# Another order of the first stages of a two-layer kernel of seven-product matrix multiplications

## The chip, the cores and the metric

The kernel runs on one core of a Trainium2 chip. The metric is the device time of one execution in microseconds (us); lower is better. One execution was also taken with the hardware profiler, and all durations below come from it. TensorE (PE) multiplies, VectorE (DVE) adds, ScalarE (ACT) scales and copies, GpSimd (POOL) and SyncE (SP) issue transfers.

## What is computed

Eight samples of 256 tokens with 1024 features go through two layers, each added to its input. Layer 0 multiplies by a matrix that depends on the sample: the common W plus the sample's mask turned into signs, times the sample's coefficient. Layer 1 picks one of eight matrices by an index.

```python
def reference(x, condB_coeff, itok_B_3_7, mask, L0_cond_W, L0_cond_b, L1_cond_weight):
    # layer 0; x is (8, 256, 1024), mask is (8, 1024, 1024) of 0 and 1
    sign = 2 * mask - 1
    y = x + einsum('bsi,oi->bso', x, L0_cond_W) + L0_cond_b \
          + einsum('bsi,bio->bso', x, sign) * condB_coeff[:, None, None]
    # layer 1
    w = L1_cond_weight[itok_B_3_7]              # (8, 1024, 1024)
    return y + einsum('bsi,boi->bso', y, w)
```

All of it is float32.

## The kernel before

**Stages.** One layer of one sample is a stage; there are 16. A 256 x 1024 by 1024 x 1024 multiplication is cut into 2 x 2 blocks on all sides and done with seven block products in place of eight (p1 to p7, in the way of Strassen and Winograd). For this, sums of blocks are formed first: s1 to s4 of the tokens (128 x 512 each, small) and t1 to t4 of the weights (a whole block each, 128 x 2048). A product is four steps of 128 in depth and fills one PSUM bank; in the profile every float32 matmul stands as two instructions. TensorE does the products of a stage in the order p1, p5, p6, p2, p7, p3, p4. Several products gather in the same bank ("u", "v", "w"); after p1 and after p6 ScalarE copies bank u out (`keep`), since later products go on adding to it, and VectorE adds banks and copies into R, the buffer of the result (`add`, L682 before).

**Layer 0** needs its matrix made: a mask block is loaded, ScalarE scales it (L525), VectorE adds the block of W (L539, "fold" in this text). R of the sample is loaded with x, and POOL adds the bias to it with an accumulating transfer (L428). When R holds y, VectorE transposes it in squares of 32 (L449) and ScalarE moves the squares to their places (L463, 16 instructions for each half), because y with features on partitions is the next stage's token operand. **Layer 1** needs no making: its four blocks are loaded as they are, by an index read on SP (L521).

**Stage 0** (layer 0 of sample 0) is done differently, without the seven products, while everything is loading: mask and W come in 11 pieces, are scaled (L308) and folded (L316), and 64 matmuls with the weights stationary give y with features on partitions (L323). ScalarE prepares x plus bias (`bias_first`, L341, eight instructions), and VectorE adds it to the four banks and so evicts them (`evict_first`, L350).

**Stage 1** was layer 1 of sample 0, the `flipped` stage: weights stationary, tokens moving in pieces of 128 columns, sixteen matmuls per product (L608). Its result comes out with features on partitions, like y, so y is added as it lies, and the sample is stored to its own output `out0`. Stages 2 and 3 are layer 0 of samples 1 and 2; from then on layer 1 of one sample and layer 0 of a later one take turns. All stages from 2 on have the tokens stationary (L618).

**What sets the order.** All work is described as tasks with a guessed length, and `plan` runs them once in a model: each engine takes, of the tasks that are ready, the one that is due first, where due times are counted back from the times at which TensorE's products should begin (HEAD = 34.5 us, then 3.435 us per product). The instructions are written out in the order of the model's starting times. On the chip each engine works its own queue strictly in that order; a wait holds up all that is behind it. Loads go through SP's queue, with eight in flight at most; weights have 11 buffers, R has 3.

Of the kernel before, what the change touches and what calls it, by code (L numbers as in the profile page):

```python
# [30 lines left out]
ORDER = ("p1", "p5", "p6", "p2", "p7", "p3")  # L31

# [16 lines left out]
LOAD, STORE, LATENCY, BEGIN = 2.50, 0.60, 2.2, 1.7  # L49
# [33 lines left out]
def plan(tasks, room, may_take):  # L83

    followers = {t: [] for t in tasks}
    for t in tasks:
        for u in t.after:
            followers[u].append(t)
    for t in reversed(tasks):
        due = [f.latest for f in followers[t]]  # L90
        own = t.latest + t.length if t.latest is not None else 1e9
        t.latest = min(due + [own]) - t.length - t.latency
    waiting = {t: len(t.after) for t in tasks}
    ready = {}
    for t in tasks:
        ready.setdefault(t.engine, [])
        if not waiting[t]:
            ready[t.engine].append(t)
    free_at = dict.fromkeys(ready, 0.0)
    free_at["DMA"] = BEGIN  # L100
    left = {}
    events, now, done = [(BEGIN, None)], 0.0, 0
    while done < len(tasks):
        for engine, queue in ready.items():
            if free_at[engine] > now + 1e-9:
                continue
            for t in sorted(queue, key=lambda t: t.latest):
                if t.earliest > now + 1e-9:
                    events.append((t.earliest, None))
                elif all(room[r.pool] > 0 for r in t.takes) and may_take(t):  # L110
                    queue.remove(t)
                    for r in t.takes:
                        room[r.pool] -= 1
                        left[r] = r.users
                    t.start, t.end = now, now + t.length + t.latency
                    free_at[engine] = now + t.length
                    if t.moves:
                        free_at["DMA"] = max(now, free_at["DMA"]) + t.moves
                        events.append((free_at["DMA"], None))
                    events += [(t.end, t), (free_at[engine], None)]  # L120
                    break
        assert events, "the plan is stuck"
        now = min(e[0] for e in events)
        for e in [e for e in events if e[0] <= now + 1e-9]:
            events.remove(e)
            t = e[1]
            if t is None:
                continue
            done += 1
            for r in t.uses:  # L130
                left[r] -= 1
                if not left[r]:
                    room[r.pool] += 1
            for f in followers[t]:
                waiting[f] -= 1
                if not waiting[f]:
                    ready[f.engine].append(f)
    order = {t: i for i, t in enumerate(tasks)}
    return sorted(tasks, key=lambda t: (round(t.start, 6), order[t]))
# [3 lines left out]
def kernel(  # L143
# [17 lines left out]
    out0: bass.AP,  # L161
# [72 lines left out]
    stages = [(0, 0), (1, 0), (0, 1)]  # L234
    for b in range(2, B):
        stages += [(0, b), (1, b - 1)]
    stages.append((1, B - 1))

    HEAD = 34.5
    owed = [0] + [3 if s == 1 else 2 for s in range(1, len(stages))]  # L240
    next_load = [0]
    loads: list[Task] = []

    def may_take(t) -> bool:
        s = getattr(t, "stage", None)
        if s is None:
            return True
        if t.engine == "DMA":
            if loads[next_load[0]] is not t:
                return False  # L250
            if room["w"] - 1 < sum(owed[: s + 1]):
                return False
            next_load[0] += 1
        else:
            owed[s] -= 1
        return True
# [132 lines left out]

    order = [(n, k, cols) for n, (k, cols) in enumerate(pieces[:-2])]  # L390
    order += [(len(pieces) - KC + k, k, ds(j * H, H)) for j in range(2) for k in (KC - 2, KC - 1)]
    last_mm = None
    mm_half = {}
    for i, (n, k, cols) in enumerate(order):
# [5 lines left out]
            takes=list(first.values()) if i == 0 else [],  # L400
            uses=([] if i == 0 else list(first.values())) + [m[k // 2], x0],
# [3 lines left out]
        mm_half[cols.start // H] = last_mm  # L405
# [33 lines left out]
    def turn(j: int, source, after, target: Buffer, opens: bool, view, moved: list):  # L439
# [25 lines left out]
        for n in range((P // Q) ** 2):  # L465
# [8 lines left out]
                    uses=[r] if takes else [r, target],  # L474
                )
# [3 lines left out]
    def stage(s: int):  # L479
        nonlocal last_mm  # L480
        layer, b = stages[s]
        final = s + 1 == len(stages)
        begin = HEAD + (s - 1) * 7 * PRODUCT
# [3 lines left out]
        if layer == 0:  # L487
            A = Buffer("a")
            got = [
                task(  # L490
                    "DMA",
                    LOAD,
                    lambda: nc.sync.dma_start(out=take(A)[:, 0:4], in_=xT[b - 1]),
                    takes=[A],
                    latency=LATENCY,
                    earliest=begin - 7 * PRODUCT,
                )
            ]
# [3 lines left out]
        flipped = s == 1  # L502
        apart = Buffer("turn")

        def part(name: str):
            if flipped and name == "s3":
                return (apart.tile if apart.tile is not None else take(apart))[:, 0].rearrange(
                    "p (k n) -> p k n", k=KH
                )
# [3 lines left out]
        def load(q: str):  # L513
            t = take(W[q])
            if layer == 0:
                nc.sync.dma_start(out=t.bitcast(I32), in_=mask[b - 1, block(q)])
# [3 lines left out]
            rows = w1_blocks[ds(rows0[b] + block(q), 1)]  # L520
            nc.sync.dma_start(out=t, in_=rows.rearrange("n p k o -> (n p) k o"))  # L521

        def scale(q: str):
            t = W[q].tile
# [4 lines left out]
        for q in BLOCKS:  # L529
            W[q] = Buffer("w")  # L530
            t = task("DMA", LOAD, lambda q=q: load(q), takes=[W[q]], latency=LATENCY)
            t.stage = s
            loads.append(t)
            if layer == 0:
                t = task("ACT", SCALE, lambda q=q: scale(q), after=[t], uses=[W[q]])
                t = task(
                    "DVE",
                    BLOCK,
                    lambda q=q: v.tensor_tensor(W[q].tile, W[q].tile, w0[q], ALU.add),  # L539
                    after=[t],  # L540
                    uses=[W[q]],
                )
            done[q] = t
        ready_r = load_r(b, begin) if layer == 0 else None

        def sum_of(what: str, after=()):
            left, op, right = SUMS[what]
            if what[0] == "s":
# [5 lines left out]
                    takes=[apart] if flipped and what == "s3" else [],  # L554
# [4 lines left out]
            fresh = what in ("t2", "t3") or (what == "t1" and s == 1)  # L559
# [26 lines left out]
        if s == 1:  # L586
            sum_of("t1")
            sum_of("t2", got)
            sum_of("t3", got)
# [11 lines left out]
        def product(name: str, a: str, w: str, bank: Buffer, opens: bool, cols=slice(0, H)):  # L601
            t = bank.tile if bank.tile is not None else take(bank)
            if flipped:
                for c in range(KH):
                    for k in range(KH):


                        nc.tensor.matmul(  # L608
                            out=t[:, ts(c, TH)],
                            lhsT=W[w].tile[:, k, ts(c, P)],  # L610
                            rhs=part(a)[:, k],
                            start=opens and c == 0 and k == 0,
                            stop=k == KH - 1,
                            skip_group_check=True,
                        )
                return
# [9 lines left out]

        def add_product(name: str, after=()):
            nonlocal last_mm
            a, w = PRODUCTS[name]
            bank = BANK[name]  # L630
# [5 lines left out]
            if flipped and a == "a11":  # L636
                needed = got[:2]
# [6 lines left out]
                uses=[A, W[w]] + ([] if opens else [r]) + ([apart] if flipped and a == "s3" else []),  # L644
# [19 lines left out]
        if flipped:  # L664
            state = {q: yT[b][1][-1] for q in BLOCKS}
# [3 lines left out]
        begun: list[str] = []  # L669

        def add(q: str, r: Buffer, op, after, get=lambda r: r.tile):
            t = R[b]
            opens = flipped and not begun
            from_y = flipped and q not in begun
            begun.append(q)

            def emit():
                to = (take(t) if opens else t.tile)[:, block(q)]
                left = to
                if from_y:  # L680
                    left = A.tile[:, block(q)].rearrange("p k n -> p (k n)")
                v.tensor_tensor(to, left, get(r), op)  # L682

# [3 lines left out]
                emit,  # L687
                after=[state[q], after, *gate, *([state[begun[0]]] if flipped and not opens else [])],
                takes=[t] if opens else [],
                uses=([] if opens else [t]) + [r] + ([A] if from_y else []),  # L690
                latest=begin + (len(mm) + 1.5) * PRODUCT,
# [10 lines left out]
        def store(q: str, cols, queue=None):  # L702
# [6 lines left out]
                    out=out0[:, block(q)] if flipped else out[b - 1, :, int(q[0]) - 1, lo:hi],  # L709
# [8 lines left out]
        copies: dict[str, tuple] = {}  # L718
# [172 lines left out]
```

## Time and profile before

| | before |
|---|---|
| time, median of 3 runs | 402.2 us (402.19 to 402.61) |
| profiled execution | 402.02 us, span 400.2 us |
| granted TensorE clock | 0.999 |
| TensorE busy | 394.2 us, 98% |
| VectorE busy | 330.6 us, 83% |
| ScalarE busy | 184.2 us, 46% |
| moved by DMA | 103.00 MB, mean 257 GB/s |

The span runs from the first to the last instruction. Busy time of TensorE includes time in which a matmul stands in the pipeline. "Start to start" is the distance of two instructions that follow each other without a gap; it is a little shorter than the duration of one. In a timeline the columns are start and length in us, engine and line, operation, operands, count, and in brackets the idle time of the engine before it with what ended it.

### The profile page before, as it was taken

The numbers are of one execution on the slowest core, as the hardware profiler recorded it, in microseconds if no ns is written. First come the engines' busy times: TensorE is split into PE (matmuls) and PEld (weight loads), VectorE is DVE, ScalarE is ACT, GpSimd is POOL, SyncE is SP. The second block draws the span as 40 slices with busy tenths as digits, with TensorE's granted clock in tenths as the row PEclk, the third lists the DMA queues.
The fourth block names the chain that finished last, engine by engine and source line by source line (L and its number), as shares of the span: only waits on it lengthen the run. The fifth ranks groups of instructions, "written<-read, shape, count | busy, mean of one in ns | idle before, by whom it ended". The sixth has DMA issues, their size and how long they took to land.

```text
span 400.2 us, 3444 instructions
## 1 busy us (share of the span) xinstructions
PE 394.2 (98%) x1155; PEld 200.0 (50%) x1155; DVE 330.6 (83%) x307; ACT 184.2 (46%) x305; POOL 27.2 (7%) x44
## 2 busy tenths in 40 slices
PE   7999999999999999999999999999999999999996
PEld 4889994444444444444444444444444444444443
DVE  2347999999999999799968998789977999668132
ACT  4552635205951496970079510993119920391000
POOL 0100011100101101010010100102001020001101
PEclk9999999999999999999999999999999999999999
DMA  8999999997873739958399573987659694601102
GB/s 256 404 414 422 418 347 388 379 338 311 189 335 111 309 113 378 318 172 317 119 397 286 209 316 125 374 236 290 235 211 345 183 376 146 273 41 53 54 0 106
DMA packets 19298, 103.00 MB, mean 257 GB/s; under 512 B 2320, under 2 KB 2832, under 8 KB 9808
## 3 DMA queue, kind: packets, MB, share of 16 engines
q1 hardware_dynamic: 14688, 87.24, 56.4%
q0 software_dynamic: 4448, 15.47, 14.6%
q8 instruction: 9, 0.15, 0.2%
q10 hardware_dynamic: 144, 0.07, 0.1%
q14 instruction: 9, 0.07, 0.1%
HBM read 94.38 MB, written 8.39 MB: 257 GB/s over the span
## 4 chain that ended last, share of the span: by engine, by line
PE 94%; DMA 4%; DVE 0%; SPq 0%; issue 0%; DVEq 0%
PE ps L618 84%; PE ps L608 6%; PE ps L323 4%; DMA w<-mask 2%; DMA w_sb<-w0T 2%; DVE w L316 0%; SPq L279 0%; SPq L286 0%; SPq L288 0%; DVE r L767 0%; DVEq L316 0%
## 5 line engine op out<-in xcount | busy, mean ns | idle before, releaser
L618 PE MATMUL ps<-w,a 128*128 128x512 f32 (+1 forms) x792 | 336.7, 588 | 0.0
L618 PEld LDWEIGHTS ps<-w,a 128*128 128x128 f32 x792 | 149.9, 190 | 186.7 <-issue 182.7
L569 DVE TENSOR_TENSOR w<-w,w 128x2048 f32<-128x2048 f32 (+1 forms) x61 | 136.8, 2252 | 3.4 <-PE ps L618 2.1
L463 ACT ACTIVATE a<-turn 32x256 f32<-32x256 f32 x224 | 92.7, 414 | 69.6 <-DVE turn L449 66.7
L539 DVE TENSOR_TENSOR w<-w,w_sb 128x2048 f32<-128x2048 f32 x28 | 64.0, 2288 | 6.1 <-ACT w L525 6.1
L682 DVE TENSOR_TENSOR r<-r,ps 128x512 f32<-128x512 f32 x73 | 49.1, 681 | 23.7 <-PE ps L618 23.5
L525 ACT ACTIVATE w<-w,cn_sb,c_sb 128x2048 f32<-128x2048 int32 x28 | 58.5, 2092 | 19.6 <-DMA w<-mask 18.8
L552 DVE TENSOR_TENSOR a<-a 128x512 f32<-128x512 f32 x59 | 39.4, 688 | 0.4
L654 ACT ACTIVATE s<-ps 128x512 f32<-128x512 f32 x15 | 8.8, 590 | 58.5 <-PE ps L618 51.2
L323 PE MATMUL ps<-a,w 128*128 128x256 f32 x128 | 29.1, 384 | 1.6 <-DMA a<-x0a 0.7
L708 POOL DMA_DIRECT2D out<-r x31 | 17.0, 549 | 199.6 <-DVE r L682 199.5
L323 PEld LDWEIGHTS ps<-a,w 128*128 128x128 f32 x128 | 23.8, 190 | 6.8 <-DVE w L316 3.1
L654 ACT ACTIVATE u<-ps 128x512 f32<-128x512 f32 x15 | 8.9, 594 | 36.7 <-PE ps L618 36.5
L316 DVE TENSOR_TENSOR w<-w,w_sb 128x512 f32<-128x512 f32 (+2 forms) x13 | 10.5, 815 | 15.6 <-DMA w_sb<-w0T 11.9
L608 PE MATMUL ps<-a,w 128*128 128x128 f32 x192 | 21.8, 275 | 0.0
L608 PEld LDWEIGHTS ps<-a,w 128*128 128x128 f32 x192 | 21.7, 192 | 0.1
L449 DVE STREAM_TRANSPOSE turn<-r 128x512 f32<-128x512 f32 x28 | 19.6, 707 | 0.6
L428 POOL DMA_DIRECT2D r<-bias x7 | 8.7, 1245 | 158.0 <-DMA r<-xR 158.0
L308 ACT ACTIVATE w<-w,cn_sb,c_sb 128x512 f32<-128x512 int32 (+2 forms) x13 | 11.6, 909 | 14.7 <-DMA w<-mask 14.7
L682 DVE TENSOR_TENSOR r<-r,s 128x512 f32<-128x512 f32 x14 | 9.6, 685 | 6.6 <-ACT s L654 6.6
L682 DVE TENSOR_TENSOR r<-r,u 128x512 f32<-128x512 f32 x14 | 9.6, 687 | 3.5 <-ACT u L654 3.4
L813 PE MATMUL idle<-zeros 128*128 128x512 bf16 (+1 forms) x11 | 3.6, 503 | 1.2 <-DVE warm L808 1.2
(24 smaller groups left out, 22.9 us busy)
## 6 DMA issues: line engine op xcount, KB each, us to landing
w<-w1T SPq DMA_DIRECT2D x32, 1024.0 KB, 9.2
w<-mask SPq DMA_DIRECT2D x28, 1024.0 KB, 10.1
out<-r POOLq DMA_DIRECT2D x31, 256.0 KB, 7.4
r<-xR SPq DMA_DIRECT2D x7, 1024.0 KB, 7.6
a<-xT SPq DMA_DIRECT2D x7, 1024.0 KB, 6.4
r<-bias POOLq DMA_DIRECT2D x7, 1024.0 KB, 15.6
w<-mask SPq DMA_DIRECT2D x5, 512.0 KB, 8.5
w_sb<-w0T SPq DMA_DIRECT2D x5, 512.0 KB, 9.0
```

The costliest lines, as they stand in the source:

```text
L323: nc.tensor.matmul(out=t.rearrange("p (c n) -> p c n", c=half)[:, c % half], lhsT=m_view(k)[:, ts(oc, P)], rhs=x0_view()[:, k], start=k == ...
L449: lambda t=t, opens=not turned: v.transpose(out=(take(r) if opens else r.tile)[:, t], in_=view(source.tile)[:, 2 * t + j]),
L463: nc.scalar.activation(to[:, :, :, f], src[:, :, :, g], AF.Copy)
L525: nc.scalar.activation(t, t.bitcast(I32), AF.Identity, bias=cn_sb[:, b : b + 1], scale=c2_sb[:, b : b + 1])
L539: lambda q=q: v.tensor_tensor(W[q].tile, W[q].tile, w0[q], ALU.add),
L552: lambda: v.tensor_tensor(part(what), part(left), part(right), op),
L569: v.tensor_tensor(to[:, rows], a, c, op)
L608: nc.tensor.matmul(out=t[:, ts(c, TH)], lhsT=W[w].tile[:, k, ts(c, P)], rhs=part(a)[:, k], start=opens and c == 0 and k == 0, stop=k == KH ...
L618: nc.tensor.matmul(out=t[:, cols], lhsT=part(a)[:, k], rhs=W[w].tile[:, k, cols], start=opens and k == 0, stop=k == KH - 1, skip_group_che ...
L654: lambda: nc.scalar.activation(take(r), bank.tile, AF.Copy),
L682: v.tensor_tensor(to, left, get(r), op)
L708: lambda: (queue or nc.gpsimd).dma_start(out=out0[:, block(q)] if flipped else out[b - 1, :, int(q[0]) - 1, lo:hi], in_=R[b].tile[:, block ...
```

## The change

- Stage 1 is now layer 0 of sample 1, and stage 2 is layer 1 of sample 0; from stage 3 on the order is as before. The flipped form is gone: all layer 1 stages have the tokens stationary.
- In the new stage 1 the mask blocks are loaded, scaled and folded in halves, in the order 11, 21, 12, 22; x comes in three transfers (a11; a12; a21 with a22), whose due times mix them with the mask halves.
- In stages 1 to 3 the products go p1, p2, p5, p6, p3, p7, p4, with banks of their own for p3 and p4. For this two more adds are made in each of these stages ("21" takes bank u after p7, "12" takes both v and p3's bank). t1 to t3 all get fresh buffers there.
- y of sample 0 lies with features on partitions. In the new stage 2 its result has tokens on partitions, so y is transposed and moved into R too (`turn`, four transposes and 32 moves more). `out0` is gone.
- Stage 0 does its last two steps in the plain order; the evictions have a start of 37.5 us or later in the plan.
- `plan` runs its model up to 150 more times with disturbed due times and keeps an order when the model's idle time of TensorE (and closeness to it) is no worse. The model's loads begin at 3.2 us, not 1.7.

In the new program VectorE's queue, from the new stage 1 on, begins: s1, s2 of stage 1; fold of 11 in two halves; s3; folds of 21 and of 12; t1 in halves; fold of 22; t2; t3; s4; t4; three evictions of stage 0; six adds into R of sample 1; the fourth eviction; two transposes of y; two adds; t1 of stage 2; and so on. On SP R of sample 1 is loaded behind the last half of 22 and ahead of W1.

The diff, cut:

```diff
-LOAD, STORE, LATENCY, BEGIN = 2.50, 0.60, 2.2, 1.7
+LOAD, STORE, LATENCY, BEGIN = 2.50, 0.60, 2.2, 3.2
+EARLY_STAGES = 3
+EARLY = ("p1", "p2", "p5", "p6", "p3", "p7")
...
-    stages = [(0, 0), (1, 0), (0, 1)]
-    for b in range(2, B):
+    stages = [(0, 0)]
+    for b in range(1, B):
         stages += [(0, b), (1, b - 1)]
     stages.append((1, B - 1))
...
+            for lo, size in ((0, 1), (1, 1), (2, 2)) if s == 1 else ((0, 4),):
+                got.append(
+                    task(
+                        "DMA",
+                        LOAD * size / 4,
...
+        halves = (ds(0, KH // 2), ds(KH // 2, KH // 2))
...
-        for q in BLOCKS:
+        for q in ("11", "21", "12", "22") if s == 1 else BLOCKS:
             W[q] = Buffer("w")
+            spans = halves if s == 1 else everything
+            for n, rows in enumerate(spans):
...
-            if flipped:
-                for c in range(KH):
-                    for k in range(KH):
-                        nc.tensor.matmul(
-                            out=t[:, ts(c, TH)],
-                            lhsT=W[w].tile[:, k, ts(c, P)],
-                            rhs=part(a)[:, k],
...
+        def bank_of(name: str):
+            return {"p3": "x", "p4": "y"}.get(name, BANK[name]) if early else BANK[name]
...
-        if flipped:
-            state = {q: yT[b][1][-1] for q in BLOCKS}
+        if layer == 1 and b == 0:
+            moved: list[Task] = []
+            for j in (0, 1):
+                turn(j, A, {t: got[2 * j : 2 * j + 2] for t in range(2)}, R[b], j == 0, as_rows, moved, None)
+                for t in range(2):
+                    state[f"{t + 1}{j + 1}"] = moved[-1]
...
+        late = 5.5 if s == 1 else None
+        for name in EARLY if early else ORDER:
             if name == "p1":
                 add_product(name)
                 copies["s1"] = keep("s1", "p1")
-                add("11", copies["s1"][0], ALU.add, copies["s1"][1])
+                add("11", copies["s1"][0], ALU.add, copies["s1"][1], due=late)
...
-                if final:
+                if final or early:
                     t = add("21", banks["u"], ALU.add, mm["p7"])
             elif name == "p3":
-                add_product(name, [v_read])
-                add("12", banks["v"], ALU.add, mm["p3"])
+                add_product(name, [] if early else [v_read])
+                if early:
+                    add("12", banks["v"], ALU.add, mm["p3"])
+                add("12", banks[bank_of(name)], ALU.add, mm["p3"])
...
+    for _ in range(ROUNDS):
+        key = list(best)
...
+        for i in range(len(tasks)):
+            if (times is None or max(lo, HEAD - 12) <= times[0][i] <= hi + 2) and rng.random() < share:
+                key[i] += rng.gauss(0.0, by)
+        found, cost = run(tasks, followers, key, room, new_gate())
+        if cost <= least:
+            best, times, least = key, found, cost
```

## The prediction

> **What bounds the kernel now.** I read the page's shares first, then the chain that ended last in order of time, then TensorE's stretches around the changed stages.
>
> ```profile
> PE 394.2 (98%) x1155; PEld 200.0 (50%) x1155; DVE 330.6 (83%) x307; ACT 184.2 (46%) x305; POOL 27.2 (7%) x44
> ...
> 21.31 14.20 PE ps L323 x64
> 35.51 25.01 PE ps L608 x224
> 60.52 336.52 PE ps L618 x792
> ```
>
> TensorE is the bound: from 21.3 to the end the chain holds nothing but matmuls. L323 is stage 0, L608 the turned stage 1, L618 the 14 other stages: 336.52 / 98 products = 3.434 us for a product, 24.04 us for a stage of seven. Stage 1 took 25.01. The stretches (PE busy, weight loads, DVE, ACT, POOL) say why:
>
> ```profile
> 36.00:42.00 6.00, 6.00 (x56) 6.00 (x55) 5.97 (x8) 1.47 (x2) 0.00 (x0) 1.00 1.01 422
> 66.00:72.00 6.00, 6.00 (x16) 2.65 (x15) 6.00 (x6) 3.35 (x4) 0.00 (x0) 1.00 1.03 427
> 90.00:120.00 30.00, 30.00 (x71) 13.19 (x70) 29.82 (x28) 21.40 (x39) 1.23 (x1) 1.00 0.80 279
> ```
>
> In stage 1 weights are loaded all the time (the second figure, 6.00 of 6.00), in stage 2 only 2.65 of 6.00. The third figure matters more: VectorE (DVE) is full from 36 to 120, and the DMA share is 1.0 until 72. So in the stages that the change rearranges TensorE leads, but VectorE and the loads are just behind, with hardly any slack. The timelines of the other engines give the prices:
>
> ```profile
> 18.67 0.33 SPq L290 DMA_DIRECT2D w_sb<-w0T  x1
> ...
> 28.58 3.28 ACT L341 ACTIVATE r<-a,b_sb 128x256 f32<-128x256 f32 x8
> 41.13 2.10 ACT L525 ACTIVATE w<-w,cn_sb,c_sb 128x2048 f32<-128x2048 int32 x1 [1.41 <-DMA w<-mask]
> ...
> 33.75 2.36 DVE L569 TENSOR_TENSOR w<-w,w 128x1024 f32<-128x1024 f32 x2 [0.89 <-DMA w<-w1T]
> ...
> 62.15 2.29 DVE L569 TENSOR_TENSOR w<-w,w 128x2048 f32<-128x2048 f32 x1
> 64.35 0.68 DVE L682 TENSOR_TENSOR r<-a,ps 128x512 f32<-128x512 f32 x1
> 64.95 0.69 DVE L552 TENSOR_TENSOR a<-a 128x512 f32<-128x512 f32 x1
> ...
> 49.22 1.27 POOL L428 DMA_DIRECT2D r<-bias  x1 [37.48 <-DMA r<-xR]
> ```
>
> Start to start on a full VectorE: 2.20 us for a whole block, 1.14 for half a block (2.36 for two, ends overlapping), 0.60 for a small one; two transposes take 1.23. The last load of stage 0 (issued at 18.67) is listed with 10.0 us to landing, so it is there at 28.67; the first block of W1 (issued at 20.04, 11.1 us) at 31.14; the first mask block, four blocks on, is scaled at 41.13. So loads land in order, one 1 MB block every 2.50 us. The bias is added into R by a transfer on POOL's queue; the times to landing of the seven are
>
> ```profile
> r<-bias POOLq DMA_DIRECT2D x7, 1024.0 KB, 15.6
> ...
> DMA to landing us min/median/max: 10.7/15.6/17.0
> ```
>
> and that of the first one, issued at 49.22 beside full load queues, is 15.6.
>
> **The turned stage goes.** 24.04 in place of 25.01: -1.0 us. Without waits stage 1 then starts at 35.5, and its fourth product, p6, at 45.8; p6 of stage 3 at 35.5 + 2 x 24.04 + 3 x 3.434 = 93.9.
>
> **The new stage 1 needs its mask scaled and folded.** The queue after stage 0 is: half of W11, a11, a21 with a22, half of W11, W21, W12, a12, W22, R, then W1. At 2.50 us per MB the last half of W11 lands at 33.1, the last of W12 at 38.1, a12 at 38.7, W22 at 41.2, R at 43.7. ScalarE does L341 until 31.9 (its place in the queue is kept), then scales the first half (1.24 us in the rows of L308): 33.1. From there VectorE has no gap: fold 11, s3, fold 21, fold 12, t1, fold 22 (five pairs of halves at 2.28 and one small) and t2 (2.29 to its end): 33.1 + 11.4 + 0.6 + 2.3 = 47.4; a few tenths of waiting for halves make it 47.6. p1, p2 and p5 find their halves in time (a12 to a tenth or two, which this hides), but p6 waits for t2 from 45.8 to 47.6: **+1.8 us**. Loads that came earlier would not help: ScalarE's 33.1 and the VectorE work behind it stand. The halves themselves are worth about one half-block of start; their four extra issues on SP (0.33 us each) lie beside a queue that is 10 us ahead.
>
> **R of sample 1 comes too late for VectorE's queue.** Before, sample 1 was worked on in stage 2, and its first add into R stood at 67.75, after the bias had landed at 49.2 + 15.6 = 64.8. Now the add into "11" stands directly behind t3, s4, t4 and three evictions of stage 0, which end near 54.5. R lands at 43.7, POOL starts 0.3 later as in the row, and the bias needs 15.6: 59.6. VectorE waits there about 5 us, and everything behind waits with it: five more adds, the last eviction, the transposes of y, t1, t2 and s2 of stage 2, then the folds of stage 3. Nothing on VectorE can pass. From this add to the end of t2 of stage 3 its queue holds 24 small instructions (14.4), 6 transposes (3.7) and 10 whole blocks (22.0): 40.2 us with the last one's tail. 59.6 + 40.2 = 99.8, where TensorE without waits would start that p6 at 93.9: **5.9 us late**, and this takes in the 1.8 above (it is the later of two limits, not a second sum). TensorE meets it in pieces: s1 of stage 2 (p5, about 1.4), s2 (p6, about 1.2), and the rest at p6 of stage 3. Behind it, up to s2 of stage 4, VectorE has 20.6 us of work and TensorE six products, also 20.6: no more is lost, but nothing is won back, since an engine that is full can't win back time for another.
>
> The bias's time is the one unknown of weight. The lowest row, 10.7, gives 54.7: VectorE then hardly waits, t2 of stage 3 ends at 94.9, and the 1.8 alone is left. The highest, 17.0, gives 61.0 and 7.3 late. I take 15.6, as that row had the same full queue beside it; the new issue, at 44.0, has four blocks of W1 and R of sample 2 behind it.
>
> [...]
>
> **The copy of y, and the smaller edits.** Four more transposes on VectorE (in the 40.2) and 32 moves on ScalarE at 0.425: 13.6 us. They start at about 65 and end, with one copy between, near 79; the scales of stage 3 follow (2.0 each, and the copy u2) until 88. VectorE comes to those folds at 81.4 to 93, each 1 us or more after its scale: hidden, with little to spare. p7 of stage 2 waits up to 0.5 us for u2's copy behind the moves; that lies within the 5.9. The own banks for p3 and p4 add two small adds in each of stages 1 to 3 (counted). Stage 0 loses its split last two steps; it ends at 35.5 as before, as stage 1 no longer needs its result. out0 goes, the stores stay as many. From stage 5 on the stages come in the old order with the old instructions, and VectorE is 3 us ahead again at the p6 of stage 5: 0.
>
> **Sum.** -1.0 + 5.9 = +4.9 on the profiled execution's 402.0 us: 406.9. (The median of the runs shown is 402.2.)
>
> **The rivals.** *The bias is quick.* 10.7 instead of 15.6, or anything under 10.5: -1.0 + 1.8 = +0.8, 402.8. For it: one row. Against it: six of seven rows are at 14.7 or more. 0.14.
> *The plan's order holds and nothing waits* (the other side): the whole -1.0, 401.0. This needs t2 of stage 1 by 45.8, so 1.8 us less VectorE work after 33.1, and the bias by 53.7. For it: VectorE is idle for over half of the time before 33. Against it: what it could do then has not landed, or waits for L341. It decides at t2: below 45.8 the kernel is faster, each us above is paid. 0.08.
> *ScalarE becomes the bound:* the 32 moves or the copies between them run later than counted, so the scales of stage 3 come after VectorE's turn. There is 1 us of slack; 2 or 3 us beyond it, or the highest bias row, give 408 to 410. 0.08.
> *The forecast,* with a bias of 14.7 to 17.0: 406.0 to 408.3. 0.70.
>
> **How the numbers follow.** The likeliest is 406.9; its own range is 405.5 to 408.5. To hold 8 in 10 the range reaches to the quick bias: 402.8 to 408.6. A measurement can tell about 0.2% (0.8 us) from no change: faster 0.08 (nothing waits), same 0.10 (most of the quick bias, which lies at that edge), slower 0.82.
>
> **What would show it.** Right: TensorE idle, first about 1.8 us near 46 on a whole-block subtraction of VectorE; VectorE idle about 5 us before 60, ended by the bias's transfer; p6 of stage 3 starting near 99.8; stage 4's start about 4.9 later than 108.6. Wrong: TensorE without a gap from 35.5 to 110 (then VectorE's prices or order are misread), a bias that lands before 55, or gaps after 125, of which this account has none.

## The result and the profile after

| | before | after |
|---|---|---|
| median | 402.23 us (402.19 to 402.61, 4 runs) | 408.38 us (407.78 to 408.76, 4 runs) |
| profiled execution | 402.02 us, span 400.2 us | 408.74 us, span 407.0 us |
| granted TensorE clock | 0.999 | 1.000 |

After against before: 1.0149, 95% interval 1.0132 to 1.0167. The changed kernel is slower by 1.5%, some 6.2 us; 406.9 was forecast.

The page's shares and its chain by engine, after:

```profile
PE 395.2 (97%) x987; PEld 185.5 (46%) x987; DVE 336.2 (83%) x321; ACT 198.6 (49%) x341; POOL 27.2 (7%) x44
...
PE 74%; DMA 14%; DVE 9%; issue 1%; SPq 1%; DVEq 0%
```

The weight loads are down by 14.5 us: the flipped stage is gone. But where the chain held nothing but matmuls from 21.3 us on, it now runs through transfers (14%) and VectorE (9%) up to 101.15 us. TensorE's timeline shows where it lets go (in brackets the idle time before the line, and what ended it):

```profile
36.66 10.61 PE L693 MATMUL ps<-w,a 128*128 128x512 f32 x24
48.92 20.84 PE L693 MATMUL ps<-w,a 128*128 128x512 f32 x48 [1.65 <-DVE w L658]
70.70 3.70 PE L693 MATMUL ps<-w,a 128*128 128x512 f32 x8 [0.94 <-DVE a L642]
75.39 7.10 PE L693 MATMUL ps<-w,a 128*128 128x512 f32 x16 [0.98 <-DVE a L642]
83.10 17.43 PE L693 MATMUL ps<-w,a 128*128 128x512 f32 x40 [0.61 <-ACT u L730]
101.15 302.53 PE L693 MATMUL ps<-w,a 128*128 128x512 f32 x712 [0.61 <-DVE w L658]
```

The five gaps stand before p6 of stage 1 (t2), p5 and p6 of stage 2 (s1, s2), p7 of stage 2 (ScalarE's copy u2) and p6 of stage 3 (t2). From there 88 products take 302.53 us, 3.438 each: not one more wait. From the start of stage 1 to the last of these gaps are 17 products, 58.4 us at 3.434, and they take 101.15 - 36.66 = 64.5: 6.1 us are lost. The brackets add up to 4.8; the rest is 0.26 per restart, because a matmul's modelled end lies that much behind the start of its follower. VectorE and POOL, which the loss comes from:

```profile
53.70 1.88 DVE L418 TENSOR_TENSOR a<-ps,r 128x512 f32<-128x512 f32 x3
60.14 0.69 DVE L757 TENSOR_TENSOR r<-r,s 128x512 f32<-128x512 f32 x1 [4.56 <-DMA r<-bias]
...
98.75 2.25 DVE L658 TENSOR_TENSOR w<-w,w 128x2048 f32<-128x2048 f32 x1
```
```profile
45.36 1.26 POOL L491 DMA_DIRECT2D r<-bias  x1 [32.58 <-DMA r<-xR]
```

R's load lands at 45.1, POOL issues the bias at 45.36, it is there 14.8 us later, and VectorE, ready at 55.6, stands until 60.14 before its first add into R. The whole-block subtraction at 98.75 is t2 of stage 3; its end, 101.0, releases the last gap.

### The profile page after: what moved, and what is told of

Read it like the earlier page. It is cut to its first block, busy times and chain, and to the rows that moved or that the text cites. A ratio compares the mean times of both kernels' runs of the same rounds, so it can differ in the third digit from the quotient of the medians.

```text
span 407.0 us, 3165 instructions
## 1 busy us (share of the span) xinstructions
PE 395.2 (97%) x987; PEld 185.5 (46%) x987; DVE 336.2 (83%) x321; ACT 198.6 (49%) x341; POOL 27.2 (7%) x44
## 4 chain that ended last, share of the span: by engine, by line
PE 74%; DMA 14%; DVE 9%; issue 1%; SPq 1%; DVEq 0%
PE ps L693 74%; DMA w<-mask 6%; DMA r<-bias 4%; DVE w L658 3%; DMA r<-xR 3%; DVE r L757 3%; DVE w L602 2%; DMA w_sb<-w0T 1%; DVE turn L512 1%; DVE a L642 1%; SPq L347 0%; SPq L354 0%; SPq L358 0%; SPq L356 0%; DVE r L840 0%
## 5 line engine op out<-in xcount | busy, mean ns | idle before, releaser
L693 PE MATMUL ps<-w,a 128*128 128x512 f32 (+1 forms) x848 | 362.2, 589 | 4.8 <-DVE w L658 2.3
L693 PEld LDWEIGHTS ps<-w,a 128*128 128x128 f32 x848 | 160.0, 190 | 207.1 <-issue 198.9
L757 DVE TENSOR_TENSOR r<-r,ps 128x512 f32<-128x512 f32 x81 | 54.3, 680 | 21.3 <-PE ps L693 20.8
L602 DVE TENSOR_TENSOR w<-w,w_sb 128x2048 f32<-128x2048 f32 (+1 forms) x32 | 64.1, 2020 | 4.6 <-ACT w L596 4.6
L596 ACT ACTIVATE w<-w,cn_sb,c_sb 128x2048 f32<-128x2048 int32 (+1 forms) x32 | 59.7, 1878 | 0.9 <-DMA w<-mask 0.4
L642 DVE TENSOR_TENSOR a<-a 128x512 f32<-128x512 f32 x60 | 40.5, 686 | 2.3 <-DMA a<-xT 1.9
L391 PEld LDWEIGHTS ps<-a,w 128*128 128x128 f32 x128 | 24.0, 191 | 7.2 <-DVE w L384 2.1
L526 ACT ACTIVATE r<-turn 32x256 f32<-32x256 f32 x32 | 13.3, 414 | 13.3 <-DVE turn L512 12.9
L757 DVE TENSOR_TENSOR r<-r,s 128x512 f32<-128x512 f32 x15 | 10.3, 684 | 11.2 <-ACT s L730 6.6
L409 ACT ACTIVATE r<-a,b_sb 128x256 f32<-128x256 f32 x8 | 3.3, 499 | 0.0
## 6 DMA issues: line engine op xcount, KB each, us to landing
r<-bias POOLq DMA_DIRECT2D x7, 1024.0 KB, 15.6
```

Of the source, the lines that this page charges most:

```text
L391: nc.tensor.matmul(out=t.rearrange("p (c n) -> p c n", c=half)[:, c % half], lhsT=m_view(k)[:, ts(oc, P)], rhs=x0_view()[:, k], start=k == ...
L526: nc.scalar.activation(to[:, :, :, f], src[:, :, :, g], AF.Copy)
L596: nc.scalar.activation(t, t.bitcast(I32), AF.Identity, bias=cn_sb[:, b : b + 1], scale=c2_sb[:, b : b + 1])
L602: v.tensor_tensor(t, t, w0[q][:, rows], ALU.add)
L642: lambda: v.tensor_tensor(part(what), part(left), part(right), op),
L693: nc.tensor.matmul(out=t[:, cols], lhsT=part(a)[:, k], rhs=W[w].tile[:, k, cols], start=opens and k == 0, stop=k == KH - 1, skip_group_che ...
```

## The experiments

The kernel before ran beside each group of experiments on the chip that these had: medians of 402.24 to 402.30 (402.23 beside the changed kernel). Each experiment's time is a median of four runs. The edits of e1 to e4, e6 to e8 and e10 are against the changed kernel, those of e5 and e9 against the kernel before.

**e1: without the first bias.** All queues keep their order; the bias of sample 1 is not added, so this is a price and not a version.

```diff
-            lambda: nc.gpsimd.dma_start(... accum_op=ALU.add),
+            lambda: nc.gpsimd.dma_start(... accum_op=ALU.add) if b > 1 else None,
```

> The changed kernel with the same order on every engine; only the accumulating transfer of the bias into R of sample 1 is left out (so sample 1 lacks its bias). Theory: VectorE's wait before the first add into R of sample 1 goes (4.6 us idle before), R itself is there near 45, and what is left is the wait of p6 in stage 1 for t2, about 1.7 us: 403.5 to 404.5 us. Rival ScalarE (the 32 moves of y's copy and the copies behind them set the pace): less than 2 us won, 406.5 or more. Rival order (the disturbed order is bad whatever the bias does): 408, no change.

Measured: 403.93 us (1.0044, 1.0027 to 1.0060). TensorE's timeline:

```profile
35.17 3.60 PE L695 MATMUL ps<-w,a 128*128 128x512 f32 x8
39.44 7.10 PE L695 MATMUL ps<-w,a 128*128 128x512 f32 x16 [0.67 <-DMA a<-xT]
48.19 152.16 PE L695 MATMUL ps<-w,a 128*128 128x512 f32 x354 [1.64 <-DVE w L660]
```

The view ends at 200 us; up to the end of the trace no further gap follows. All gaps behind stage 1 are gone, and 4.4 of the 6.2 us with them: that is what one transfer costs that lands 4.6 us after VectorE wants it. The edit also takes 1 MB of traffic away, but none of the five gaps of the changed kernel was ended by a load, and e6 wins part of this with the transfer kept. What is left, 1.7 us over the kernel before, is stage 1 itself (p6 starts 13.0 us after the stage instead of 10.3, so 2.7 lost) less the 1.0 that the flip gives back.

**e2: without the search** (`ROUNDS = 0`), so with the plan's first order.

> The changed kernel with 0 rounds of search. The unsearched order has the adds into R of sample 1 at nearly the same place, behind two evictions, and R at the same place in the load queue; from that add to s2 of stage 3 its VectorE queue holds 41.3 us where the searched one has 40.2 to t2. Theory: the same loss, 407.5 to 409. Rival order (the search has made it worse): 406 or less.

Measured: 410.16 us (1.0193, 1.0176 to 1.0210), above the range that I had given. The search did not bring the loss; it wins 1.8 us against its own starting point. VectorE waits 4.21 us for the bias in this order too, until 59.61, since the plan believes in 8.5 us for the transfer with or without the search; behind that, p6 of stage 3 waits for s2, which stands behind t2 here, until 101.92 (100.59 in e4, which got the bias at the same time), and p7 another 0.45 us for a copy. TensorE also waits 2.29 us for s1 of stage 1, but that lies under the wait for the bias.

**e3: the plan is told the truth about the bias** (`latency` 8.5 to 14.5), **and t2 of stage 1 is made in halves.**

```diff
-            latency=8.5,
+            latency=14.5,
...
-            if s == 1 and what == "t1":
+            if s == 1 and what in ("t1", "t2"):
```

> The changed kernel, planned with a bias that takes 14.5 us instead of 8.5 after its issue, and t2 of stage 1 made in halves. In the order that comes out R is loaded one block later, and 30 us of VectorE work stand ahead of the first add into it, so VectorE finds it landed. VectorE's work from the first fold to t2 of stage 3 is 63.0 us from 33.1 (96.1), against TensorE's 93.9 plus what p6 of stage 1 waits (its first half of t2 comes 14.3 us after 33.1, so still 1.7): theory 403 to 404. Rival ScalarE: 405.5 or more, since its moves and scales stay. Rival: the halves alone cost or win, then within 1 us of 408.

Measured: 405.74 us (1.0083, 1.0066 to 1.0100), some 2 us above what I had expected. VectorE waits for the bias no more, and still t2 of stage 3 is late:

```profile
48.66 48.30 PE L693 MATMUL ps<-w,a 128*128 128x512 f32 x112 [0.38 <-DVE w L658]
98.24 27.29 PE L693 MATMUL ps<-w,a 128*128 128x512 f32 x63 [1.28 <-DVE w L658]
```

VectorE has no gap of note from 33.8 to there. TensorE loses 4.4 us in all: 2.9 in stage 1, where p6 starts 13.2 us after the stage, and 1.5 before p6 of stage 3. So the wait for the bias is a large part of the changed kernel's loss, but the queue around it is full in this order too.

**e4: a short copy of y.** Each half's 16 moves on ScalarE become one plain copy (y of sample 0 comes out mixed up).

```diff
+            if target is R[0]:
+                if f == g == 0:
+                    nc.scalar.activation(view(target.tile)[:, j:4:2], r.tile, AF.Copy)
+                return
```

> The changed kernel with the same order; the 32 moves of y's copy into R of sample 0 are replaced by one plain copy for each half (two instructions, about 1.2 us each, so the values land unturned and sample 0 comes out mixed up). ScalarE gets 11 us less to do in stage 2. Theory: VectorE's queue sets the pace, ScalarE only fills a gap of TensorE that is paid anyway: 407.8 to 408.7, no change. Rival ScalarE: 407 or less.

Measured: 408.12 us (1.0139, 1.0122 to 1.0157). The gap behind ScalarE's copy disappears (0.61 before), the next one grows from 0.61 to 1.35, and the time stays. The moves cost nothing here: whichever of them is late, VectorE's t2 is later.

**e5: the turn alone.** The kernel before with its stage order and planner; only stage 1 has its tokens stationary, and y is turned into R for it. The stage's adds wait for the last of the 32 moves.

```diff
+        if s == 1:
+            for j in (0, 1):
+                read += turn(j, A, {t: got[2 * j : 2 * j + 2] for t in range(2)}, R[b], j == 0, as_rows, moved)
...
-            state = {q: yT[b][1][-1] for q in BLOCKS}
+            state = {q: moved[-1] for q in BLOCKS}
```

> One part of the change alone: the order of stages, the planner and the loads of the kernel before, but layer 1 of sample 0 with the tokens stationary like every other stage, and y turned into R by four transposes on VectorE and 32 moves on ScalarE. Theory (VectorE's and ScalarE's queues set the first stages in this order too): 1.0 us less for the products (24.04 for 25.01), but p5 of stage 1 waits about 1.4 us, since two transposes (0.6 us each) stand before the second half of t1 and s1, and p6 up to 1 more for the copy of p1, which stands behind 27 moves of 0.42 us; then the adds into R wait for the last move and the second stage's t1 is some 2 us later than before, without much left of it at the products: 402.0 to 403.8, taken 402.8. Rival (turning y costs nothing, the flip's 1.0 us is won): 401.0 to 401.5.

Measured: 408.53 us (1.0139, 1.0108 to 1.0170): far above both. The four executions differ, and with them the mean granted clock of TensorE: 407.10 us at 1.000, 407.93 at 0.996, 409.14 and 409.16 at 0.992. The one profiled is 409.14. ScalarE's timeline has one part of the reason:

```profile
34.41 11.50 ACT L462 ACTIVATE r<-turn 32x256 f32<-32x256 f32 x27 [2.35 <-DVE turn L448]
45.93 0.60 ACT L636 ACTIVATE s<-ps 128x512 f32<-128x512 f32 x1
```

The copy of p1, for which p6 waits, stands behind 27 moves, and TensorE is idle for 3.10 us. The stretches around it (busy time of TensorE, weight loads, VectorE, ScalarE and GpSimd, each with its count; then TensorE's clock, the DMA share and GB/s) have the other:

```profile
44.00:45.57 1.57, 0.00 (x0) 0.00 (x0) 1.57 (x3) 1.52 (x5) 0.00 (x0) 1.00 1.03 423
45.57:52.40 6.83, 5.82 (x7) 2.52 (x8) 2.87 (x5) 5.09 (x8) 1.27 (x1) 0.50 1.01 421
52.40:54.00 1.60, 1.60 (x5) 0.72 (x4) 1.60 (x1) 0.81 (x2) 0.00 (x0) 1.00 1.02 379
```

For 6.83 us the granted clock is half, and 5.82 us of work are done at that rate: 2.9 us that no wait shows. With the three waits (0.66, 3.10, and 0.51 for a move at 115.48), 0.8 for their restarts and the flip's -1.0 the sum is 7.0; this execution is 6.9 above the kernel before. The execution at full clock, 2.0 us faster, is still 4.9 above it.

**e6: the late bias in the plan alone**, with R's load held where it was.

```diff
-            earliest=begin - 8 * PRODUCT,
+            earliest=begin - 8 * PRODUCT if b > 1 else begin + 2.0,
...
-            latency=8.5,
+            latency=14.5,
```

> The changed kernel, with a bias transfer that the plan takes for 6 us longer (14.5 for 8.5) and the load of R of sample 1 held where it was, behind all of stage 1's loads; nothing else changed, so that the plan puts the adds into R of sample 1 behind y's evictions, two transposes, a small sum and t1 of stage 2. Theory (the wait for bias is the larger part of the loss, and behind it VectorE has still no slack): VectorE reaches the first add near 61.3 and waits no more than 0.5 us; p6 of stage 1 starts some 3 us late (three small sums stand before t1 and t2), and p6 of stage 3 0 to 0.5 more: 403.7 to 405.3, taken 404.5. Rival (the wait for bias is all there is): 401.0 to 402.5. Rival (the wait is paid whatever the order, since the second stage needs the adds): 407.5 or more.

Measured: 405.84 us (1.0081, 1.0059 to 1.0104); the first add starts at 61.32 without a wait. TensorE's timeline (the view ends at 125 us):

```profile
35.43 10.79 PE L693 MATMUL ps<-w,a 128*128 128x512 f32 x24
48.93 62.04 PE L693 MATMUL ps<-w,a 128*128 128x512 f32 x144 [2.71 <-DVE w L658]
111.92 13.57 PE L693 MATMUL ps<-w,a 128*128 128x512 f32 x31 [0.95 <-ACT a L526]
```

2.5 us come back by order alone, and p6 of stage 1 now waits 2.71 us: the theory but for 1.3 us over my figure. Nearly all of that is a wait for ScalarE's moves of sample 1 (0.95 us at 111.9) with its restart, which I had not looked for.

**e7: small sums on GpSimd.** e6, and s1 to s4 of stages 1 to 3 go from VectorE to GpSimd.

```diff
-                    "DVE",
-                    SMALL,
-                    lambda: v.tensor_tensor(part(what), part(left), part(right), op),
+                    "POOL" if early else "DVE",
+                    1.2 if early else SMALL,
+                    lambda: (nc.gpsimd if early else v).tensor_tensor(part(what), part(left), part(right), op),
```

> As the run with the late bias, and the four small sums of tokens in each of the stages 1 to 3 are made by GpSimd instead of VectorE (12 operations of 0.6 us less in VectorE's queue). Theory (VectorE's queue is the bound over stages 1 to 3): no product of stage 2 or 3 waits for VectorE; p6 of stage 1 still starts about 2 us late, since its blocks are loaded, scaled and folded only by about 45: 402.5 to 403.8, taken 403.2. Rival (GpSimd's sums take over 3 us each, or slow VectorE's): s1 and s2 come late for p5 and p6 of stage 1, 404.5 or more. Rival (VectorE is not the bound): same as the run with the late bias, within 0.5 us.

Measured: 411.32 us (1.0218, 1.0196 to 1.0239). The rival came true, by its second half. POOL's and VectorE's timelines of the same stretch:

```profile
41.01 8.45 POOL L642 TENSOR_TENSOR a<-a 128x512 f32<-128x512 f32 x4 [29.68 <-DMA a<-xT]
```
```profile
37.09 3.49 DVE L602 TENSOR_TENSOR w<-w,w_sb 128x1024 f32<-128x1024 f32 x3
40.50 3.43 DVE L658 TENSOR_TENSOR w<-w,w 128x1024 f32<-128x1024 f32 x2
43.85 4.48 DVE L602 TENSOR_TENSOR w<-w,w_sb 128x1024 f32<-128x1024 f32 x2
```

GpSimd needs 2.1 us for a sum of 0.60. Worse, VectorE's half-blocks, 1.14 us each at first (three in 3.49), take 2.24 each at 43.85, while GpSimd adds. p6 of stage 1 waits 5.15 us instead of 2.71, the clock is at 0.50 for 6.83 us, from 49.07 (4.15 us of work), and two more waits follow at 130 and 138 us (0.37 and 1.39). t2 of stage 1 ends at 51.6 where it ended at 48.8 in e6, although four sums have left the queue. What GpSimd's sums would take alone, no run shows.

**e8: e7, with ScalarE's bias of stage 0 behind the scales of stage 1, and t2 of stage 1 in halves.**

```diff
-    biased = task("ACT", 3.3, bias_first, after=[last_scale], takes=[xb], uses=[x0])
+    biased = task("ACT", 3.3, bias_first, after=[last_scale], takes=[xb], uses=[x0], earliest=HEAD + 6.0)
```

> As the run with the sums on GpSimd, and two edits for stage 1: ScalarE adds stage 0's bias (eight operations, 3.3 us) behind the scales of stage 1's blocks instead of before them, and t2 of stage 1 is made in halves. Theory (stage 1's p6 then waits for the loads alone: the last half of block 22 lands near 42.6, scale 1.1, fold 1.1, half of t2 1.2 put t2 at about 46.0 against 45.5): 401.4 to 402.5, taken 401.9; faster than the kernel before by 0.3 or so. Rival (ScalarE is no part of it): as the run with the sums on GpSimd, less 1.1 at most.

Measured: 411.17 us (1.0215, 1.0194 to 1.0236), the same as e7: nothing can be told about the edit under GpSimd's disturbance. p6 starts 1.0 us sooner (50.73), and the time does not follow: at 94.82 TensorE waits 0.96 us for a fold of VectorE, which it does not in e7, and at 130 us both are level again.

**e9: e5 with a sooner copy.** The adds into the left half of R wait for the first 16 moves only.

```diff
-            state = {q: moved[-1] for q in BLOCKS}
+                    turned_y[f"{t + 1}{j + 1}"] = moved[-1]      # after each turn
+            state = dict(turned_y)
```

> As the run with the turn alone (408.5), but the adds into the two left blocks of R wait for the first 16 moves only and not for all 32, which makes the plan put the copy of p1 behind 19 moves instead of 27. Theory (in that run TensorE stood idle for 3.10 us before p6, which alone cost 3.1 us more, because the granted clock fell to 0.50 from about 45.8 to 52.2; an idle time of 2.71 us in the run with the late bias cost no clock): the copy is ready near 43.1 against 42.4, so p6 waits some 0.7 us and the clock stays at 1.00; of the 6.2 us that stall and clock gave VectorE and ScalarE, about 2 come back as waits of p5 and p6 of stage 2: 402.0 to 404.5, taken 403.2. Rival (the low clock has nothing to do with the idle time): the clock falls again, and 405.5 or more.

Measured: 407.88 us (1.0141, 1.0125 to 1.0158). p6 of stage 1 waits 0.62 us, as worked out, and the clock stays whole there. But p5 of stage 2 then waits 2.10 us for s1, and

```profile
66.50:67.42 0.92, 0.55 (x2) 0.34 (x3) 0.92 (x2) 0.38 (x1) 0.46 (x1) 1.00 1.07 432
67.42:70.84 3.42, 3.42 (x6) 1.34 (x5) 3.42 (x4) 2.09 (x1) 0.00 (x0) 0.50 1.00 411
70.84:72.00 1.16, 1.16 (x4) 0.52 (x3) 1.16 (x1) 0.00 (x0) 0.97 (x2) 1.00 1.04 434
```

the clock falls again, 0.55 us after TensorE went back to work. So the length of the idle time is not the rule: 2.10 us were followed by a stretch of 3.42 (1.7 us of work), and 2.71 in the profiled execution of e6 by none. My figure was 4.7 us too low: 1.7 for the clock, and 2.3 because the waits came to 3.9 us and 1.1 for four restarts, where I had counted 2.7 in all; 0.7 lies in the count that I started from. Added to the kernel before instead, the parts give the median: 402.3 - 1.0 + 5.0 + 1.7 = 408.0. The profiled execution (408.54, the slowest of the four) also began stage 1 0.6 us later than e5 (36.08). With or without the better place of the copy, the turn alone does not pay: the flipped stage cost 1.0 us, and what replaces it needs VectorE, which is full there, and ScalarE, whose moves stand before its copies.

**e10: e6 with the scales first.** The two edits of e8 (the plan holds ScalarE's bias back to HEAD + 10.0 here), with all small sums on VectorE.

> As the run with the late bias (405.8), and the two edits for stage 1 with all small sums on VectorE: stage 0's bias on ScalarE behind the scales of stage 1's blocks, t2 of stage 1 in halves. Theory (VectorE's folds of stage 1 start about 2 us earlier, near 31.5 for 33.7, once ScalarE's 3.3 us of bias no longer stand before the scales): p2 waits up to 0.7 us for its piece of x and p6 about 0.5 (2.71 in the run with the late bias); VectorE's queue is then full up to t1 of stage 3, which is 0 to 1.2 us late: 402.5 to 404.6, taken 403.6. Rival (the loads set stage 1, and ScalarE's place costs nothing): p6 waits 2 us or more, 405.0 or more.

Measured: 404.28 us (1.0051, 1.0034 to 1.0067).

```profile
39.56 7.11 PE L693 MATMUL ps<-w,a 128*128 128x512 f32 x16 [0.98 <-DMA a<-xT]
47.31 3.67 PE L693 MATMUL ps<-w,a 128*128 128x512 f32 x8 [0.64 <-DVE w L658]
51.25 41.60 PE L693 MATMUL ps<-w,a 128*128 128x512 f32 x96 [0.27 <-DVE a L642]
93.34 306.02 PE L693 MATMUL ps<-w,a 128*128 128x512 f32 x720 [0.49 <-DVE w L658]
```

Within the range given. VectorE's first fold starts at 31.68 instead of 33.69; p6 of stage 1 waits 0.64 instead of 2.71 and starts 12.3 us after the stage instead of 13.5, although p2 now waits 0.98 for its piece of x. What t2 in halves gives to this was not separated. This is the best version that leaves nothing out: 4.1 us better than the changed kernel, and still 0.5% slower than the kernel before. No version that was run beats that one.

## Why the prediction was right, and by how much its terms were off

The time lies in the forecast's own range, close to its upper end, and the mechanism is the one forecast: p6 of stage 3 hangs on VectorE's queue, and that on the bias of sample 1. By the prediction's own steps:

- **The flip.** -1.0 holds for the products: TensorE takes 3.438 us for each after, against 3.434 in the other stages before. No run shows this microsecond by itself; where the turn alone was made (e5, e9) the turning cost more than it.
- **p6 of stage 1, +1.8.** Too small: 2.7 in e1 and 3.0 in e4, where stage 1 begins at 35.2 and 35.1 and p6 starts at 48.2 and 48.4 in place of 47.6; 2.0 in the profiled run of after (48.92 - 36.66 less 10.3), where the stage begins late. The chain from the first fold to t2 was forecast from 33.1; the fold starts at 33.59 in e1 and at 34.31 in after. The term left out s1 and s2, which stand ahead of that fold and wait for x (after):

```profile
32.98 1.42 DVE L642 TENSOR_TENSOR a<-a 128x512 f32<-128x512 f32 x2 [1.92 <-DMA a<-xT]
34.31 2.44 DVE L602 TENSOR_TENSOR w<-w,w_sb 128x1024 f32<-128x1024 f32 x2
```

  ScalarE, which was given as the reason, ends its first scale at 34.04 here, 0.3 sooner, so the two limits lie close together. That its bias before the scales costs time is shown by e10 against e6, where the folds come before s1 and s2. The piece a12, to which I gave "a tenth or two", makes p2 wait 0.67 in e1 and 0.88 in e4; that is hidden, since p6 waits for t2 in any case. In after the whole term is hidden under the next, as forecast.
- **The bias, +5.9.** R landed at 45.1, not 43.7; the transfer took 14.8, not 15.6; the add began at 60.14, not 59.6; from it to the end of t2 of stage 3 passed 40.8 us, not 40.2, in part because two adds from PSUM in a row took up to 1.48 us where I counted 1.2. So p6 of stage 3 began at 101.15, not 99.8: 1.35 us, which are nearly all of the 1.5 between forecast and median.

  e4 has the same order and separates them: there the add began at 59.63, as forecast, VectorE's queue again took 40.8, and p6 of stage 3 began at 100.59. So 0.8 of the 1.35 is VectorE's queue with the step from t2 to p6, and this is the mis-sized term; about 0.5 is scatter: in the profiled run of after a mask piece of stage 0 landed 1.3 us later than before, and the bias was issued at 45.36; in e2, e4 and e10 it was issued at 44.8, in the same or nearly the same order of loads.

  That the add began on the forecast in e4 is luck in part: the bias was issued 0.8 later than I had it, from my count of 2.50 us per MB from a landing at 28.67 (which of the two was off was not separated), and its transfer was 0.8 shorter. Nor is its time a constant: the seven transfers of before took 10.7 to 17.0 us, those of after 14.8 to 16.6, and the first of e3 15.1, beside full load queues like the first of after. Whether an earlier R would have brought the bias sooner, no run shows.
- **Stage 0 ends at 35.5.** 36.66 in the profiled run, 35.1 to 35.5 in e1 to e8: scatter of the start and not the change. It is not what made the forecast low either: e4, where stage 1 starts 1.5 us sooner than in after, has p6 of stage 3 at 100.59 and 408.12 us. An earlier start only makes the wait longer, because the bias is tied to the loads and not to TensorE.
- **The copy of y: no more than 0.5, inside the 5.9.** Its gap was 0.61, a little more, and e4 shows that it is inside.
- **Nothing lost after stage 3:** right, 302.53 us without a gap.

The rivals: *the quick bias* was priced at 402.8; the nearest run to it, e1, gave 403.9, because stage 1 costs 2.7 and not 1.8. *Nothing waits* (401.0) was never reached, not even by e10. *ScalarE as the bound* is refuted by e4 for this order. What the prediction did not see is how much of the loss was a wrong number in the plan: with 14.5 us in place of 8.5, and R's load held where it was, the same model makes an order that is 2.5 us faster (e6).

## What to carry to other kernels

An order that is searched for in a model is only as good as the durations in it: take them from the trace, under the load of the place where they are used, before adding rounds of search. Behind a full queue a late transfer cost nearly all of its wait here (4.4 of 4.56 us, e1), so put what depends on it as far back as it will go, and look for the engine that feeds the queue (here ScalarE's scales) rather than for another engine to share the work. And a change that replaces an awkward form has to be charged for what the regular one needs: in e5 and e9 four transposes and 32 moves in the one stretch that has no slack cost more than the 1.0 us of the flipped stage.

## What the runs showed of the hardware

- **The clock after a wait.** In the profiled executions, stretches of granted clock 0.50 came in lengths of 6.83 (e5, idle for 3.10 us), 6.83 (e7, 5.15), 3.40 (e8, 4.10) and 3.42 us (e9, 2.10); none after 2.71 (e6) or 2.29 (e2). So the two long ones are twice as long as the two short ones, and the length of the idle time alone does not separate the cases: the clock fell after 2.10 us (e9) and not after 2.71. In e5 the fall came 2.1 us after TensorE's last matmul, in e8 and e9 when it was already at work. It also changes between executions of one kernel: the mean clock of e5's four was 0.992, 0.992, 0.996 and 1.000, and two of the four of e6 and of e2, not the profiled ones, show 0.994 or 0.995, where the other two show 0.999 or 1.000. So it is not settled that a wait of 2.71 or 2.29 us costs no clock; where those executions lost it, no trace shows. What decides between a fall and none was not shown.
- **GpSimd beside VectorE:** 1.14 us to 2.24 for a half-block of VectorE, and 2.1 to 2.8 us for a small sum on GpSimd (four in 8.45 beside half-blocks, four in 11.2 in stage 2).
- **The start scatters:** stage 1 began between 34.98 us (e10) and 36.66 us (after) from the first instruction, and in e4, whose loads are those of after, at 35.12.
